# A decoder layer on one Trainium2 core: query norms by selector products, paired 64x64 products, and two sums moved off VectorE

## The chip, the core and the metric

The kernel runs on one core of one Trainium2 chip. The core has TensorE (PE in the profile, with its weight loads listed apart as PEld), VectorE (DVE), ScalarE (ACT), GpSimd (POOL) and a queue of DMA issues on SyncE (SP). The metric is the device time of one execution in microseconds; lower is better.

## The reference, cut to what matters

The layer takes x of 4 sequences with 512 tokens of width 512. It adds three parts to x, each after a layer norm: a gated delta-rule attention with 16 heads, a routed cross-attention over 64 context rows, and a feed-forward block with ternary weights. The change touches the first part alone:

```python
q = _causal_conv_silu(hidden_states @ Wq, conv_q).reshape(B, T, H, DK)   # DK = 96, 4 taps
k = _causal_conv_silu(hidden_states @ Wk, conv_k).reshape(B, T, H, DK)
v = _causal_conv_silu(hidden_states @ Wv, conv_v).reshape(B, T, H, DV)   # DV = 192
q = _l2norm(q) * DK ** (-0.5)                # divides by the root of the sum of squares
k = _l2norm(k)
...
def step(S, inp):                            # over 512 tokens, for every head
    q_t, k_t, v_t, g_t, b_t = inp
    S = S * jnp.exp(g_t)[..., None, None]
    kv = jnp.einsum('bhk,bhkv->bhv', k_t, S)
    delta = (v_t - kv) * b_t[..., None]
    S = S + jnp.einsum('bhk,bhv->bhkv', k_t, delta)
    o = jnp.einsum('bhk,bhkv->bhv', q_t, S)
    return (S, o)
...
o = o * jax.lax.rsqrt(var + EPS) * norm_weight * jax.nn.silu(gate)
return o.reshape(B, T, VAL_DIM) @ Wo         # and x = x + that
```

## The kernel before, in words

The attention is worked in 16 steps: 4 sequences, and for each of them 4 groups of 4 heads. The recurrence over tokens is done in 4 chunks of 128 tokens. Inside a chunk the delta rule is a triangular system, whose inverse is built once per step.

A step has these stages. `keys` projects the key channels of 4 heads in 3 tiles of 128 channels (96 of one head, and a third of the fourth head in the other 32), applies the four convolution taps and SiLU, transposes the keys to get their norms, and forms key-by-key products `lm`, masked by decays. `invert` inverts the triangular blocks: 32x32 blocks by substitution on VectorE (31 rounds of a product and a reduction), then the 32-wide and 64-wide off-diagonal blocks by small products on TensorE. `queries` projects the queries in the same way, takes their sums of squares (`ssq`) and forms key-by-query products. `pair` runs twice per step, each for two heads: `values` projects 3 value tiles, takes taps and SiLU, and turns them from channels to tokens by 32x32 transposes on VectorE, a store to DRAM and a load back; `gates` projects the gates; then the chunks follow in order, with the state in SBUF, and each chunk's output is normed, gated, turned through DRAM and multiplied by `Wo`, and the product is added to the residual tile `x`.

`project` is the helper of all convolved projections: four products of 128x512 in f32 accumulate in a PSUM bank, ScalarE writes the last tap's product to an `acc` tile, and VectorE adds the three other taps straight from PSUM.

Nothing is issued in the order of the source. Every operation is recorded by `Recorder.record` with an estimated cost and with its dependences, and `Recorder.order` plays the recorded operations through a list scheduler: for each engine it takes the ready operation that can start first, and among equals the one that is due first. Due times come from the step number (times `PERIOD`; keys and inversion of the next step count as `LEAD` steps later) and from a table `SHIFT` of offsets by stage and engine. Tiles live in numbered slots (6 for `acc`, 3 PSUM banks `mm`, 2 `tp`, 3 `ch`), and an operation that needs a slot waits in the plan till one is free. Operations in a `rec.group()` stay together. Then `emit` writes each engine's instructions in the planned order; on the chip each engine runs its own list strictly in that order. All these instructions carry line L558, where `emit` calls them, and so a line tells nothing here: groups are told apart by tile names and shapes.

`busywork` looks for gaps of TensorE in the plan that are longer than `IDLE` (0.8 us) and fills them with 128x128 products on a free PSUM bank, which nobody reads. They carry line L556.

```python
n = int((min(o.start - at, most) - IDLE) / each)
```

An f32 product shows as two PE instructions (two passes); a transpose as one.

Of the kernel before, what the change touches and what calls it, by code (L numbers as in the profile page):

```python
# [41 lines left out]
PERIOD = 133.9  # L42
LEAD = 6.21
PERIOD2 = 6.0
IDLE = 0.8
TERNARY = 7
# [3 lines left out]
    "ffn": -286.8,  # L50
    "ffn gpsimd": -630.6,
    "ffn scalar": 95.3,
    "ffn tensor": 9.6,
    "ffn vector": -751.6,
    "gate": -14.6,
    "gate scalar": 309.8,
    "gate tensor": 70.8,
    "head": -371.9,
    "head gpsimd": 602.6,
    "head scalar": 531.6,  # L60
    "head tensor": 307.0,
    "head vector": 293.4,
    "inv": 43.3,
    "inv gpsimd": -20.4,
    "inv scalar": -59.4,
    "inv tensor": -18.8,
    "inv vector": -64.7,
    "keys": 84.4,
    "keys gpsimd": 118.7,
    "keys scalar": 1126.6,  # L70
    "keys tensor": -205.3,
    "keys vector": -169.0,
    "out": 93.1,
    "out gpsimd": 163.4,
    "out scalar": 284.7,
    "out tensor": 136.0,
    "out vector": -605.5,
    "query": 22.7,
    "query gpsimd": -0.2,
    "query scalar": -194.1,  # L80
    "query tensor": -15.6,
    "query vector": -235.0,
    "rec": -229.1,
    "rec scalar": -429.1,
    "rec tensor": -1099.0,
    "rec vector": -319.3,
    "route": -26.3,
    "route gpsimd": 158.5,
    "route scalar": -304.1,
    "route tensor": -259.5,  # L90
    "route vector": 422.0,
    "tern": -187.4,
    "tern scalar": 56.9,
    "tern tensor": 115.4,
    "tern vector": 686.3,
    "value": -352.2,
    "value scalar": 287.9,
    "value tensor": -1023.7,
    "value vector": -417.0,
    "wo": 128.6,  # L100
    "wo scalar": -58.9,
# [200 lines left out]
class Op:  # L302
    __slots__ = ("engine", "calls", "cost", "tail", "deps", "nexts", "bufs", "due", "step", "table",
                 "waits", "start", "end", "index", "ready", "nbytes", "stage")


class Recorder:
# [18 lines left out]
    def group(self):  # L326
        return Group(self)

    def record(self, engine, method, args, kw):
        outs = [args[0]] + ([kw["accum_out"]] if "accum_out" in kw else [])  # L330
        ins = [x for x in list(args[1:]) + [v for k, v in kw.items() if k != "accum_out"]
               if isinstance(x, (View, bass.AP))]
        if self.grouped is not None and self.grouped.calls:
            op = self.grouped
            assert op.engine == engine
        else:
            op = self.grouped if self.grouped is not None else Op()
            op.engine, op.calls, op.cost, op.deps, op.nexts = engine, [], 0.0, set(), []
            op.bufs, op.step, op.table, op.index, op.nbytes = [], self.step, None, len(self.ops), 0
            op.stage = self.stage  # L340
            self.ops.append(op)
        op.calls.append((method, args, kw))
        op.cost += self.cost(op, engine, method, args, kw, outs, ins)
        for b in self.held:
            self.use(op, b)
        self.held = []
        ins += self.needed
        self.needed = []
        for x in ins:
            self.touch(op, x, False)  # L350
        for x in outs:

            self.touch(op, View(x.buf) if engine == "tensor" else x, True)
# [69 lines left out]
    def order(self, period, shift):  # L423
# [11 lines left out]
        for o in ops:  # L435
            o.due += shift.get(o.stage, 0.0) + shift.get(f"{o.stage} {o.engine}", 0.0)
# [87 lines left out]
    def busywork(self, banks, weights, moving, most=99.0):  # L524


        each = self.cost(None, "tensor", "matmul", (None, weights, moving), {}, [moving], [])
        use = {}
        for o in self.done:
            for b in o.bufs:  # L530
                if b.slots in banks:
                    t = use.setdefault((b.slots, b.slot), {}).setdefault(b, [o.start, o.end])
                    t[1] = max(t[1], o.end)
        fill, at = {}, 0.0
        for o in self.done:
            if o.engine != "tensor":
                continue
            n = int((min(o.start - at, most) - IDLE) / each)
            free = [k for k, u in use.items() if all(t[1] < at or o.start < t[0] for t in u.values())]
            if n > 0 and free:  # L540
                fill[o] = free[0][0].tiles[free[0][1]], n
            at = o.start + o.cost
        return fill
# [27 lines left out]
class Group:  # L571


    def __init__(self, rec):
        self.rec = rec
# [6 lines left out]
    def __exit__(self, *exc):  # L582
        self.rec.grouped = None
# [3 lines left out]
def decoder_layer(ctx: ExitStack, tc: tile.TileContext, a: dict, out: bass.AP):  # L587
# [7 lines left out]
    w.vs = dram.tile([NB, NHG, T, GV], F32, name="vs")  # L595
    w.os = dram.tile([NB, NHG, NC, GV, P], F32, name="os")
# [69 lines left out]
def attention(w, a):  # L666
# [38 lines left out]
    t_k = slots("k", 8, [DK, T])  # L705
    t_q = slots("q", 5, [DK, T])
# [13 lines left out]
    t_j = slots("j", 1, [P, NC * DK], ordered=False)  # L720
    t_oq = slots("oq", 1, [P, HG * DV])
# [99 lines left out]
    def project(wsrc, hT, taps):  # L821


        w = t_w(P, KC, P)
        sp.dma_start(w, wsrc)
        pp = p_mm(P, T)
        acc = t_acc(P, T)
        for kc in range(KC):
            rec.hold(acc)
            pe.matmul(pp, w[:, kc], hT[:, kc], start=kc == 0, stop=kc == KC - 1)  # L830
        act.activation(acc, pp, AF.Copy, scale=taps[:, 3:4])
        for j in range(1, 4):
            dve.scalar_tensor_tensor(
                acc[:, j:], pp[:, : T - j], taps[:, 3 - j : 4 - j], acc[:, j:], ALU.mult, ALU.add
            )
        return acc, w

    def project4(key, f, hT, taps, t_dst):


        dst = [t_dst(DK, T) for _ in range(4)]
        for i in range(3):
            rec.hold(*dst)
            acc, _ = project(a[key][f, i], hT, taps[:, i])
            act.activation(dst[i], acc[:DK], AF.Silu)
            act.activation(dst[3][32 * i : 32 * i + 32], acc[DK:P], AF.Silu)
        return dst

    def keys(s, f):
# [4 lines left out]
        k = project4("wk", f, s["hT"], cqk[:, 0, f], t_k)  # L854
# [3 lines left out]
        for j in range(4):  # L858
            pk = p_tp(P, NC, DK)
            rec.hold(kt[j])  # L860
            with rec.group():
                for c in range(NC):
                    pe.transpose(pk[:, c], k[j][:, c * P : (c + 1) * P], ident[:DK, :DK])
# [27 lines left out]
        for j in range(4):  # L891
            pa = p_tp(P, NC, P)
            rec.hold(lm)
            rec.need(dec[j])
            with rec.group():
                for c in range(NC):
                    cs = slice(c * P, (c + 1) * P)
                    pe.matmul(pa[:, c], k[j][:, cs], k[j][:, cs], start=True, stop=True)
            dve.tensor_tensor(lm[:, j], pa, dec[j], ALU.mult)
        return s  # L900

    def invert(s):
# [48 lines left out]
        for n0 in range(0, NPR, 8):  # L951
            p0 = p_tp(P, 8, 64)
            rec.hold(tb)
            with rec.group():
                for n in range(8):
                    pe.matmul(
                        p0[64:128, n], lm[0:64, n0 + n, 64:128], xa[:, n0 + n], start=True, stop=True
                    )
            act.copy(tb[64:128, n0 : n0 + 8], p0[64:128])
        for n0 in range(0, NPR, 8):  # L960
            p1 = p_tp(P, 8, 64)
            with rec.group():
                for n in range(8):
                    pe.matmul(
                        p1[0:64, n], tb[64:128, n0 + n], lm[64:128, n0 + n, 64:128], start=True, stop=True
                    )
            act.copy(lm[0:64, n0 : n0 + 8, 64:128], p1[0:64])

    def queries(s, f):

        rec.stage = "query"
        q = project4("wq", f, s["hT"], cqk[:, 1, f], t_q)
        s["q"] = q
        ssq = s["ssq"] = t_s(P, 4, NC)
        for j in range(4):
            pk = p_tp(P, NC, DK)
            with rec.group():
                for c in range(NC):
                    pe.transpose(pk[:, c], q[j][:, c * P : (c + 1) * P], ident[:DK, :DK])
# [4 lines left out]
        for j in range(4):  # L984
            pa = p_tp(P, NC, P)
            rec.need(s["lm"][:, j])
            with rec.group():
                for c in range(NC):
                    cs = slice(c * P, (c + 1) * P)
                    pe.matmul(pa[:, c], s["k"][j][:, cs], q[j][:, cs], start=True, stop=True)  # L990
            dve.tensor_tensor(s["dec"][j], pa, s["dec"][j], ALU.mult)

    def values(s, hg, jo):
# [3 lines left out]
        for vt in range(NVT):  # L997
            rec.hold(*vo)
            acc, w = project(a["wv"][hg, vt], s["hT"], cv[:, hg * NVT + vt])
# [29 lines left out]
    def pair(s, hg, jo, last):  # L1029
# [13 lines left out]
        for c in range(NC):  # L1043
# [3 lines left out]
            if c:  # L1047
                pr, rz = p_ch(P, HG, DV), t_rz(P, HG, DV)
                rec.hold(rz)
                for j in range(HG):  # L1050
                    pe.matmul(pr[:, j], k[jo + j][:, cs], st[:, j], start=True, stop=True)
# [25 lines left out]
            if c:  # L1077
                pq, oq = p_ch(P, HG, DV), t_oq(P, HG, DV)
                rec.hold(oq)
                for j in range(HG):  # L1080
                    pe.matmul(pq[:, j], q[jo + j][:, cs], st[:, j], start=True, stop=True)
# [39 lines left out]
            dve.tensor_add(x, x, py)  # L1121
# [326 lines left out]
def layouts(i):  # L1448
# [20 lines left out]
    def halves(wm):  # L1469
# [10 lines left out]
        "xid": substitution_start(),  # L1480
        "wv": by_tile(i[n + "Wv"], P).reshape(NHG, NVT, P, KC, P),
# [35 lines left out]
```

## Time and profile before

| what | value |
|---|---|
| median of 3 runs | 2442.74 us (2439.18 to 2442.87) |
| the profiled execution, its own time | 2443.09 us |
| its span, first to last instruction | 2441.3 us |
| mean granted TensorE clock | 0.988 |
| TensorE busy | 2354.8 us, 96% |
| VectorE busy | 1940.5 us, 79% |
| ScalarE busy | 1331.2 us, 55% |
| GpSimd busy | 856.3 us, 35% |
| filler products on L556 | 746 passes |

A group's line gives line, engine, operation, tiles out and in, shapes and count, then busy time and mean time of one, then the engine's idle time just before and what ended it. [...] The first 200 us are the start of the pipeline, the last 240 us are routing and feed-forward, and between them a step takes about 134 us.

### The profile page before, as it was taken

To read this page: it belongs to the slowest core of one execution; us is meant where nothing else is said; L and a number is where in the kernel's file an instruction comes from. 1 tells how busy PE (TensorE), PEld (TensorE's weight loads), DVE (VectorE), ACT (ScalarE), POOL (GpSimd) and SP (SyncE) were. 2 spreads that over 40 slices of the span, in tenths; PEclk is the share of its full clock that TensorE was granted. 3 is DMA by queue.
4 is the path that set the end of the run, shared out by engine and by line. 5 is a ranking of instruction groups with operands and counts; after the bars stand their busy time and mean duration, and the time that the engine had idled before them with its cause. 6 is when DMAs were issued, how large, how long until landed. Compare 5 with 4: busy or idle time off the path is not lost.

```text
span 2441.3 us, 38049 instructions
## 1 busy us (share of the span) xinstructions
PE 2354.8 (96%) x12976; PEld 1478.7 (61%) x12976; DVE 1940.5 (79%) x3594; ACT 1331.2 (55%) x2807; POOL 856.3 (35%) x1275
## 2 busy tenths in 40 slices
PE   8989999999999999999999999999999999999988
PEld 5576566666565756565664756665657575644455
DVE  4978797979696979788869889898979796587764
ACT  3746456555455575747553656455364554655553
POOL 2332333233333232314122333333223422376663
PEclk9989999999999999999999999999999999999999
DMA  5547343535353455556664545554544445431000
GB/s 167 148 117 192 84 114 74 129 82 159 90 156 90 129 145 149 146 154 163 163 171 104 142 111 137 152 146 127 153 125 118 112 110 157 115 81 60 22 18 18
DMA packets 579009, 294.76 MB, mean 121 GB/s; under 512 B 424000, under 2 KB 495936, under 8 KB 578560
## 3 DMA queue, kind: packets, MB, share of 16 engines
q1 hardware_dynamic: 578816, 292.34, 45.7%
q8 instruction: 103, 1.69, 0.3%
q14 instruction: 90, 0.74, 0.1%
HBM read 223.93 MB, written 68.29 MB: 120 GB/s over the span
## 4 chain that ended last, share of the span: by engine, by line
PE 72%; DVE 15%; ACT 6%; POOL 3%; issue 2%; DMA 1%; SPq 0%; POOLq 0%; DVEq 0%; ACTq 0%
PE mm L558 45%; PE ch L558 16%; DVE mem L558 15%; PE tp L558 10%; ACT mem L558 5%; POOL mem L558 3%; ACT L558 1%; PE tp L556 1%; DMA vs<-mem 0%; PE ch L556 0%; DMA mem<-vs 0%; SPq L558 0%; DMA mem<-in_wg 0%; DMA mem<-in_cst 0%; PE mm L556 0%
## 5 line engine op out<-in xcount | busy, mean ns | idle before, releaser
L558 PE MATMUL mm<-mem 128*128 128x512 f32 (+4 forms) x3760 | 1527.1, 543 | 20.1 <-issue 6.7
L558 PEld LDWEIGHTS mm<-mem 128*128 128x128 f32 (+1 forms) x3504 | 627.2, 190 | 536.5 <-issue 399.0
L558 POOL TENSOR_TENSOR mem<-mem 128x2 f32<-128x2 f32 (+5 forms) x864 | 714.3, 839 | 671.5 <-ACT mem L558 464.5
L558 ACT ACTIVATE mem<-mem 128x192 f32<-128x192 f32 (+6 forms) x1361 | 674.4, 524 | 454.9 <-DVE mem L558 307.0
L558 DVE SCALAR_TENSOR_TENSOR mem<-mm,mem 128x511 f32<-128x511 f32 (+4 forms) x656 | 463.5, 728 | 168.2 <-ACT mem L558 144.3
L558 PE MATMUL ch<-mem 128*128 128x192 f32 (+3 forms) x2688 | 547.9, 342 | 30.8 <-DVE mem L558 18.9
L558 PEld LDWEIGHTS ch<-mem 128*128 128x128 f32 (+2 forms) x2176 | 367.1, 188 | 151.0 <-issue 44.2
L558 PEld LDWEIGHTS tp<-mem 32*32 32x32 f32 (+3 forms) x5462 | 322.3, 137 | 137.4 <-issue 61.2
L558 PE MATMUL tp<-mem 32*32 32x32 f32 (+7 forms) x5782 | 371.5, 225 | 23.9 <-ACT mem L558 15.0
L558 DVE TENSOR_REDUCE mem<-mem 128x4 f32<-128x384 f32 (+32 forms) x660 | 332.7, 506 | 64.2 <-POOL mem L558 33.5
L558 POOL TENSOR_SCALAR mem<-mem 128x1 f32<-128x1 f32 (+3 forms) x352 | 121.3, 345 | 576.3 <-ACT mem L558 378.5
L558 DVE STREAM_TRANSPOSE mem<-mem 128x384 f32<-128x384 f32 (+3 forms) x368 | 279.8, 763 | 50.9 <-ACT mem L558 24.0
L558 DVE TENSOR_TENSOR mem<-mem 128x64 f32<-128x64 f32 (+31 forms) x553 | 250.2, 454 | 16.5 <-POOL mem L558 1.9
L558 ACT ACTIVATE mem<-mm,mem 128x512 f32<-128x512 f32 x192 | 130.1, 682 | 189.0 <-PE mm L558 188.0
L558 ACT COPY mem<-tp 32x512 f32<-32x512 f32 (+6 forms) x292 | 172.3, 603 | 83.7 <-PE tp L558 80.8
L558 DVE SCALAR_TENSOR_TENSOR mem<-ch,mem 128x192 f32<-128x192 f32 (+1 forms) x272 | 128.4, 508 | 49.9 <-PE ch L558 44.9
L558 PEld LDWEIGHTS <-mem 128*128 128x128 bf16 x1088 | 92.1, 98 | 119.9 <-ACT mem L558 16.7
L558 ACT ACT_TABLE_LOAD x114 | 146.3, 1283 | 30.1 <-DVE mem L558 27.6
L558 DVE TENSOR_TENSOR mem<-mem,mm 128x512 f32<-128x512 f32 x144 | 97.0, 678 | 46.5 <-PE mm L558 44.7
L558 DVE TENSOR_TENSOR mem<-tp,mem 128x512 f32<-128x512 f32 (+1 forms) x132 | 87.0, 666 | 44.0 <-PE tp L558 26.6
L558 ACT COPY mem<-ch 128x384 f32<-128x384 f32 x128 | 60.8, 475 | 92.6 <-PE ch L558 91.9
L558 ACT ACTIVATE mem<-mm 128x384 f32<-128x384 f32 x128 | 61.9, 488 | 84.2 <-PE mm L558 83.5
(33 smaller groups left out, 772.6 us busy)
## 6 DMA issues: line engine op xcount, KB each, us to landing
mem<-in_wg SPq DMA_DIRECT2D x32, 768.0 KB, 4.6
mem<-in_wv SPq DMA_DIRECT2D x96, 256.0 KB, 3.0
mem<-wos SPq DMA_DIRECT2D x96, 256.0 KB, 3.2
vs<-mem SPq DMA_DIRECT2D x384, 64.0 KB, 2.7
mem<-vs SPq DMA_DIRECT2D x128, 192.0 KB, 3.5
os<-mem SPq DMA_DIRECT2D x512, 48.0 KB, 2.6
mem<-os SPq DMA_DIRECT2D x128, 192.0 KB, 2.9
mem<-gs SPq DMA_DIRECT2D x64, 256.0 KB, 4.7
```

The source lines that it names most:

```text
L556: engine.matmul(bank[:, : m.shape[1]], w, m, start=True, stop=True)
L558: getattr(engine, method)(*[real(x) for x in args], **{k: real(v) for k, v in kw.items()})
```

## The change

Four edits to the computation's placement, and a new plan.

1. Query norms: the query tiles are no longer transposed for their sums of squares. ScalarE squares the three projected tiles in place, three products with a 128x32 selector `sel` (ones in column 0 for the first 96 rows, in column 1 for the last 32) sum over channels on TensorE, each into its own 32 rows of one PSUM bank, and the sums go to DRAM and come back with tokens on partitions.
2. The four groups of eight 64x64 products in `invert` become three: the middle one interleaves the second product of the first half with the first product of the second half.
3. In the value projections (`F = 1`) the tap of offset 3 is multiplied by ScalarE out of PSUM into the weight tile and added by GpSimd, in place of VectorE's third tap.
4. The product with `Wo` is copied out of PSUM by ScalarE and added to `x` by GpSimd (`HP = 1`).

A group may now state its cost for the planner; `SHIFT` has entries by stage, engine and output tile; `PERIOD`, `LEAD` and all offsets are other numbers; and no filler is put ahead of TensorE's first operation. The SiLU of the first three key and query tiles now covers all 128 rows.

```diff
-PERIOD = 133.9
-LEAD = 6.21
+PERIOD = 137.5
+LEAD = 10.97
+QN = 1
+F = 1
+HP = 1
 ...
-            n = int((min(o.start - at, most) - IDLE) / each)
+            n = int((min(o.start - at, most) - IDLE) / each) if at else 0
 ...
     def __exit__(self, *exc):
+        if self.cost is not None:
+            self.rec.grouped.cost = self.cost
 ...
-    def project(wsrc, hT, taps):
+    def project(wsrc, hT, taps, split=False):
 ...
         act.activation(acc, pp, AF.Copy, scale=taps[:, 3:4])
-        for j in range(1, 4):
+        if split:
+            last = w.rearrange("p k c -> p (k c)")
+            act.activation(last[:, 3:], pp[:, : T - 3], AF.Copy, scale=taps[:, 0:1])
+        for j in range(1, 3 if split else 4):
             dve.scalar_tensor_tensor(
                 acc[:, j:], pp[:, : T - j], taps[:, 3 - j : 4 - j], acc[:, j:], ALU.mult, ALU.add
             )
+        if split:
+            pool.tensor_add(acc[:, 3:], acc[:, 3:], last[:, 3:])
 ...
-            acc, _ = project(a[key][f, i], hT, taps[:, i])
-            act.activation(dst[i], acc[:DK], AF.Silu)
+            acc, _ = project(a[key][f, i], hT, taps[:, i], F > 1 and key == "wq" or F > 2)
+            act.activation(dst[i], acc, AF.Silu)
 ...
-        for n0 in range(0, NPR, 8):
-            p0 = p_tp(P, 8, 64)
-            with rec.group():
-                for n in range(8):
-                    pe.matmul(
-                        p0[64:128, n], lm[0:64, n0 + n, 64:128], xa[:, n0 + n], start=True, stop=True
-                    )
-            act.copy(tb[64:128, n0 : n0 + 8], p0[64:128])
-        for n0 in range(0, NPR, 8):
-            p1 = p_tp(P, 8, 64)
-            with rec.group():
-                for n in range(8):
-                    pe.matmul(
-                        p1[0:64, n], tb[64:128, n0 + n], lm[64:128, n0 + n, 64:128], start=True, stop=True
-                    )
-            act.copy(lm[0:64, n0 : n0 + 8, 64:128], p1[0:64])
+        for n0 in (0, 8, 16):
+            pi = p_tp(P, 8, 64)
+            with rec.group(0.94):
+                for n in range(8):
+                    if n0 < NPR:
+                        m = n0 + n
+                        pe.matmul(pi[64:128, n], lm[0:64, m, 64:128], xa[:, m], start=True, stop=True)
+                    if n0:
+                        m = n0 - 8 + n
+                        pe.matmul(
+                            pi[0:64, n], tb[64:128, m], lm[64:128, m, 64:128], start=True, stop=True
+                        )
+            if n0 < NPR:
+                act.copy(tb[64:128, n0 : n0 + 8], pi[64:128])
+            if n0:
+                act.copy(lm[0:64, n0 - 8 : n0, 64:128], pi[0:64])
 ...
+        if QN:
+            pq = p_tp(P, T)
+            for i in range(3):
+                act.activation(accs[i], q[i], AF.Square)
+            with rec.group(0.9):
+                for i in range(3):
+                    pe.matmul(pq[32 * i : 32 * i + 32], sel, accs[i], start=True, stop=True)
+            act.copy(accs[0][:DK], pq[:DK])
+            there = w.qs[s["b"], f]
+            for i in range(3):
+                sp.dma_start(there[2 * i : 2 * i + 2], accs[0][32 * i : 32 * i + 2])
+            sums = t_sums(P, 3, 2, NC)
+            for i in range(3):
+                sp.dma_start(sums[:, i], there[2 * i : 2 * i + 2].rearrange("h (c p) -> p h c", p=P))
+            dve.tensor_copy(ssq[:, 0:3], sums[:, :, 0])
+            dve.tensor_reduce(ssq[:, 3], sums[:, :, 1].rearrange("p i c -> p c i"), AX.X, ALU.add)
-        for j in range(4):
+        for j in range(0 if QN else 4):
 ...
-            acc, w = project(a["wv"][hg, vt], s["hT"], cv[:, hg * NVT + vt])
+            acc, w = project(a["wv"][hg, vt], s["hT"], cv[:, hg * NVT + vt], F > 0)
 ...
-            dve.tensor_add(x, x, py)
+            if HP:
+                y = t_acc(P, D)
+                act.copy(y, py)
+                pool.tensor_add(x, x, y)
+            else:
+                dve.tensor_add(x, x, py)
```

## The prediction, made before the changed kernel ran

> **What bounds the kernel now.** I read the page's busy times and slices first, then the answer by stretches, the groups with shapes kept apart, the waits of TensorE (PE), and last the timeline of single groups.
>
> ```profile
> span 2441.3 us, 38049 instructions
> PE 2354.8 (96%) x12976; PEld 1478.7 (61%) x12976; DVE 1940.5 (79%) x3594; ACT 1331.2 (55%) x2807; POOL 856.3 (35%) x1275
> PE 72%; DVE 15%; ACT 6%; POOL 3%; issue 2%; DMA 1%; SPq 0%; POOLq 0%; DVEq 0%; ACTq 0%
> ```
>
> PE is busy for 96% of the span and holds 72% of the chain that ended last; VectorE (DVE) comes second, ScalarE (ACT) and GpSimd (POOL) have room. The stretches (length, then busy us of PE, weight load, DVE, ACT, POOL; clock) show the shape:
>
> ```profile
> 60.00:194.00 134.00, 122.05 (x820) 92.28 (x819) 118.55 (x212) 84.67 (x160) 51.15 (x59) 0.94 0.48 137
> 596.00:730.00 134.00, 132.69 (x716) 80.86 (x717) 104.38 (x192) 69.45 (x153) 42.63 (x64) 1.00 0.46 117
> 1266.00:1400.00 134.00, 123.68 (x682) 79.85 (x682) 115.61 (x217) 68.89 (x152) 41.46 (x55) 0.96 0.46 118
> ```
>
> A step in the middle is PE alone: 1.3 us of 134 are idle. The first step and a dip at 1266 lose 10 to 12 us each. Part of "busy" is filler (L556: products nobody reads, put where the planner sees a gap). The filler alone, by start, middle, end:
>
> ```profile
> 0.00:200.00 200.00, 34.70 (x266) 33.72 (x266) 0.94 0.49 146
> 200.00:2200.00 2000.00, 28.78 (x210) 27.15 (x210) 0.99 0.50 129
> 2200.00:2442.00 242.00, 32.69 (x270) 31.72 (x270) 1.00 0.09 30
> ```
>
> 746 filler passes, 96 us. All of DVE's 1940 us can therefore shrink without moving the end by more than what PE waits for DVE:
>
> ```profile
> PE ch L558 <- DVE mem L558: 18.9, 20, 4.6
> PE tp L558 <- ACT mem L558: 15.0, 28, 1.9
> PE ch L558 <- ACT mem L558: 10.8, 18, 1.3
> PE tp L558 <- DVE mem L558: 7.8, 11, 1.2
> ```
>
> With two smaller lines (mm after ACT 6.6, after DVE 4.8) that is 31.5 us behind DVE and 32.4 us behind ACT, of 2441.
>
> **PE's own work.** The pace comes from timeline rows, since listed durations overlap (start, length, count):
>
> ```profile
> 41.75 0.50 PE L558 MATMUL tp<-mem 96*128 96x96 f32 x4
> 1109.28 1.20 PE L558 MATMUL tp<-mem 32*32 32x32 f32 x64
> 1110.41 7.13 PE L558 MATMUL mm<-mem 128*128 128x512 f32 x16
> 1120.63 1.11 PE L558 MATMUL tp<-mem 64*64 64x64 f32 x16 [0.67 <-ACT mem L558]
> 1342.99 2.17 PE L556 MATMUL tp<-mem 128*128 128x128 f32 x18
> ```
>
> Take one listed duration off the length and divide by the steps. A 512-wide pass: (7.13-0.60)/15 = 0.435 us; an f32 product is two passes. A 96-row transpose (one pass): (0.50-0.25)/3 = 0.083. A 64x64 pass: (1.11-0.22)/15 = 0.059, so a group of 8 products 0.94. A filler pass: (2.17-0.27)/17 = 0.112. A 32x32 pass, with products on two different corners of the array taking turns: (1.20-0.19)/63 = 0.016; single starts there come in couples 7 ns apart, 24 ns between couples. The second pass of one product thus runs beside the first pass of the next, and starts stay in order.
>
> 1. Query norms. 16 transposes a step go: 256 x 0.083 = -21.2 us. Added: three products 32 columns wide, 512 long, on three column groups, x16. No row shows this form. Fully side by side they take 2 x 0.435 = 0.87 us, one after another 2.61. By the corner rows (a pass of one beside a pass of the next, in order) it is 4 passes, 1.74 us. I take 1.74: +27.8 us (ends 13.9 and 41.8). [...] Entering and leaving the narrow form: the product after the 64x64 group starts 0.09 us late, x32 = +2.9 (ends 0 and 6).
> 2. Pairing. Four groups of 8 become 8, 16 interleaved, 8 on opposite corners. By the corner rows the interleaved 16 take about as long as 8 alone: -0.94 x 16 = -15.0 us (ends -16 and 0). The price: the second half's first product now waits in one group with the first half's second; its cover is the next step's projections, as now.
> 3. Filler. In the emitted order of the changed program I count 900 passes against 746: start 164 (266), middle 516 (210), end 220 (270). Difference +154 x 0.112 = +17.2 us. The 82 at the very start go; cold, they took 10.98 us, not 9.2: -1.6. The cold clock then falls on real work instead: +2. In the middle alone it is +34 us, with two runs of 55 and 80 products ahead of a pair's output products and recurrence. There the planner gave PE nothing else; the step's chain (taps, sum, SiLU, turn, store, load, scale) has to be waited out.
> 4. DVE's work, cost by the groups (count | busy, mean ns of one):
>
> ```profile
> L558 DVE SCALAR_TENSOR_TENSOR mem<-mm,mem 128x509 f32<-128x509 f32 x192 | 139.0, 741 | 3.9
> L558 DVE TENSOR_TENSOR mem<-mem,mm 128x512 f32<-128x512 f32 x144 | 97.0, 678 | 46.5 <-PE mm L558 44.7
> L558 POOL TENSOR_TENSOR mem<-mem 128x512 f32<-128x512 f32 x208 | 247.1, 1218 | 75.2 <-DVE mem L558 73.3 <-ACT mem L558 1.4
> L558 ACT ACTIVATE mem<-mm,mem 128x512 f32<-128x512 f32 x192 | 130.1, 682 | 189.0 <-PE mm L558 188.0
> ```
>
> DVE loses 96 taps x 0.741 = 71, 128 residual sums x 0.678 = 87, 64 query reductions x 0.547 = 35; 32 small ones come (0.2 each): -187 us, to 72%. ACT gains 96 x 0.682 = 65, 128 copies x 0.581 = 74, 16 copies = 9; its squares change from 64 x 0.488 to 48 x 0.649 (even); 19 table loads fewer x 1.283 = -24: +124, to 60%. POOL gains 224 x 1.218 = +273, to 46%. All this is hidden by PE, except in PE's waits. DVE's wait of 31.5 us falls with its load; between the first step (DVE 88%, PE idle 12) and a middle step (78%, idle 1.3) it falls faster than the load, so I take a quarter: -8. ACT's 32.4 grows by its 9%: +3. Bounds: -31 and +30.
>
> [...]
>
> ```profile
> L558 DVE TENSOR_TENSOR mem<-mem 128x480 f32<-128x480 f32 x16 | 12.1, 753 | 0.5
> ```
>
> This takes 753 ns where the 512-wide one with a PSUM input takes 678, about 108 over its size, with POOL's wide sums on 20% of the span; the change makes that 32%. [...]
>
> 5. Queues. SP issues 97 more DMAs at 0.43 us: 42 us of a queue that waits most of the time. The three loads of norms carry 1024 four-byte pieces each; four-byte packets take 9 ns here, so 192 per engine are 1.7 us a step, ahead of value loads. Behind SP's wait for the norms' copy stand value stores. POOL's new sum waits for both ACT and DVE, and behind it stand the gates and norms of the output stage; DVE's turn waits for it through SiLU. On a value tile's chain that is one ACT pass off DVE's 0.74 and 1.2 more on POOL, +0.5 us a tile, hidden behind two or three tiles in flight.
> 6. A lower row count for slots (accumulators kept for squares and residual copies, 6 in all) shows in the emitted order as the filler of point 3; not counted twice.
>
> Sum: -21.2 + 27.8 + 2.9 - 15.0 + 17.2 - 1.6 + 2 - 8 + 3 = +7.1. Span 2441.3 + 7.1 = 2448.4; the profiled execution took 2443.09, 1.8 more than its span (the median shown is 2442.74, 0.35 less than it): 2450.2, I say 2450. PE's net saving is 5 us where the planner's costs (0.168 a transpose, 0.9 for the three narrow products) promise far more, and the middle's filler eats it.
>
> **Rivals.**
> A. DVE's waits go. Place: recurrence products behind DVE (18.9 us) and the first step, where 81 fillers and then 2 us of waiting stand ahead of the inversion. If three quarters of 31.5 us vanish (-24 in place of -8) and the first step sheds another 12 us of idle PE to look like a middle step, it is 2450 - 16 - 12 = 2422. For it: DVE is 88% busy where PE idles most, and the start has 102 filler passes fewer. Against: in the middle PE has only 45 us idle in 2000, and 306 filler passes (34 us) are added there. It decides from 12 us of relief on beyond my 5, where the result passes 2438.
> B. The value chain becomes the bound: POOL's sum stands behind gate and norm work in a strict order, and each of 32 pairs enters its recurrence 1.2 us later with nothing for PE to do: +38, 2488. For it: those two long filler runs say PE already runs out of work there. Against: POOL at 46%.
> C. The narrow products overlap fully: -14, 2436; or not at all: +14, 2464. Small either way, and inside the forecast's range.
> That the change doesn't do what it says: the emitted order shows all four parts, 256 transposes fewer and 48 narrow products.
>
> **Numbers.** Runs differ by 0.15%, so 0.2% (4.9 us: 2437.9 to 2447.6) is what a measurement can tell. Forecast with C around it: 0.54, own range 2436 to 2466, of which slower 0.41, same 0.10, faster 0.03. A: 0.34, faster 0.31, same 0.03. B: 0.12, slower. Together: faster 0.34, same 0.13, slower 0.53. Both signs weigh, so the range runs from A's far side, 2412, to B's near side, 2484.
>
> **What would show it.** Right: PE still at 96%; 16 groups of six narrow passes of about 1.7 us; interleaved 64x64 passes near 0.03 us apart; filler 900 passes and near 110 us, more in the middle; DVE near 1750, ACT near 1455, POOL near 1130. A is right if PE's waits behind DVE fall under 10 us and a stretch from 60 to 194 has PE over 128. B is right if PE waits behind ACT or DMA for over 60 us ahead of recurrence products. Wrong as a whole: middle steps of 130 us or less, or narrow groups over 2.6 us.

## The result, and the profile after

The changed kernel takes 2498.86 us (median; 2494.19 to 2500.04) against 2442.8 for the kernel before: ratio 1.0229, 95% interval 1.0211 to 1.0247. The forecast had the sign and not the size: 2450, with a range to 2484. The page of the changed kernel (its real instructions carry line L675, the filler L673):

```profile
span 2492.4 us, 38312 instructions
...
PE 2368.0 (95%) x12970; PEld 1467.0 (59%) x12970; DVE 1809.1 (73%) x3338; ACT 1432.0 (57%) x3012; POOL 1153.5 (46%) x1499
...
PE 39%; DVE 15%; ACT 5%; POOL 3%; issue 2%; DMA 1%; SPq 0%; POOLq 0%; DVEq 0%; ACTq 0%
```

ACT and POOL are near the forecast (1455 and 1130). DVE is 59 us above it (1750): it was relieved of 131 us, not 187. The shares of the chain add up to 65% only, so it was followed through a part of the span and is not read further. Here are the same three stretches as before (length, then busy us of PE, weight load, DVE, ACT, POOL; clock, DMA share, GB/s):

```profile
60.00:194.00 134.00, 121.47 (x793) 87.85 (x792) 117.29 (x230) 88.59 (x182) 55.15 (x66) 0.97 0.54 146
596.00:730.00 134.00, 130.03 (x716) 81.56 (x716) 92.55 (x170) 75.48 (x166) 56.01 (x68) 0.99 0.48 121
1266.00:1400.00 134.00, 124.04 (x692) 78.96 (x692) 115.70 (x209) 76.03 (x167) 58.89 (x69) 0.97 0.54 134
```

PE's idle time in the middle step rises from 1.3 to 4.0 us while DVE's work there falls by 12. PE idles more behind an engine that has less to do. The waits of PE say behind which engine (total us, times, longest; `ch`, `tp` and `mm` are the PSUM banks that PE writes):

```profile
PE ch L675 <- DVE mem L675: 44.7, 34, 5.3
PE tp L675 <- DVE mem L675: 17.7, 14, 7.6
PE ch L675 <- ACT mem L675: 13.7, 26, 0.7
...
PE mm L675 <- DVE mem L675: 9.9, 13, 2.0
```

Behind DVE it is 72.3 us instead of 31.5; behind ACT (with 10.6 for tp and 8.0 for mm) 32.3 instead of 32.4. The filler alone, as before in start, middle and end, has the 900 passes that were counted:

```profile
0.00:200.00 200.00, 20.16 (x164) 19.27 (x164) 0.98 0.56 163
200.00:2200.00 2000.00, 60.41 (x506) 59.67 (x506) 0.98 0.50 126
2200.00:2494.00 294.00, 27.89 (x230) 27.13 (x230) 1.00 0.12 39
```

PE's own edited work, from the timeline (start, length; x6 means that six passes are merged in one row):

```profile
98.00 1.06 PE L675 MATMUL tp<-mem 128*32 128x512 f32 x6
98.99 0.91 PE L675 MATMUL mm<-mem 128*128 128x384 f32 x2
```

and the 64x64 products among the groups with shapes apart:

```profile
L675 PE MATMUL tp<-mem 64*64 64x64 f32 x1024 | 55.2, 221 | 0.8 <-ACT mem L675 0.8
```

Six narrow passes are through after 0.99 us: the three first passes start within 14 ns, the three second ones 0.45 us later. Start to start, the 48 narrow products take 16.4 us in all, 1.03 a step (0.99 in 15 steps, 1.60 in the last).

**Where a state copy waits.** Timeline of the changed kernel, where PE's longest wait behind a recurrence sum lies:

```profile
1066.16 3.22 POOL L675 TENSOR_TENSOR mem<-mem 128x512 f32<-128x512 f32 x2 [14.69 <-ACT mem L675]
...
1067.32 0.94 DVE L675 TENSOR_TENSOR mem<-mem 128x432 f32<-128x432 f32 x1
...
1068.93 0.94 DVE L675 TENSOR_TENSOR mem<-mem 128x448 f32<-128x448 f32 x1
...
1070.56 0.64 DVE L675 TENSOR_TENSOR mem<-mem 128x464 f32<-128x464 f32 x1
...
1074.70 0.69 DVE L675 TENSOR_TENSOR mem<-mem 128x512 f32<-128x512 f32 x1
1075.31 1.01 DVE L675 COPY mem<-ch 96x384 f32<-96x384 f32 x2
...
1075.92 1.33 PE L675 MATMUL ch<-mem 96*128 96x192 f32 x3 [5.29 <-DVE mem L675]
```

Two things are to be seen. PE has waited 5.29 us for the copy of the state, which stands in DVE's strict order behind rounds of the next step's substitution. And under GpSimd's two sums (1066.16 to 1069.38) a round's product takes 0.94 us; after them a larger one takes 0.64. The stretch makes only some 0.6 us of this wait of 5.29, an estimate from these rows. I paired all SBUF products of DVE with what GpSimd did beside them. Against the fast fifth (20th percentile) of their own shapes they are 407 ns longer where a 128x512 GpSimd sum covers most of them (51 products), 420 under a 128x384 one (26), and 0 with GpSimd idle (311). Sums out of PSUM, reductions and transposes hardly move (5, 2 and 20 ns under the 128x512 sums; 4, 4 and 20 with GpSimd idle). Summed over all of DVE's instructions, the time above that floor is 70 us before and 98 after; that is the excess in what follows.

**Planned and late.** The kernel's own planner gives each operation a start. I paired DVE's instructions in order with the profile. "Plan" is the planner's last end in us, "late" the median of profile start less planned start over the last 60 instructions. The kernel before: plan 2397, late 44. The changed one: plan 2403, late 90. The lateness grows by 5 to 19 us per 200 us of plan, up to 1600. So the loss is 6 us of plan and 46 us of running late against it. The experiments are to say why.

### The profile page after: what moved, and what is told of

Read it like the earlier page. It is cut to its first block, busy times and chain, and to the rows that moved or that the text cites. A ratio compares the mean times of both kernels' runs of the same rounds, so it can differ in the third digit from the quotient of the medians.

```text
span 2492.4 us, 38312 instructions
## 1 busy us (share of the span) xinstructions
PE 2368.0 (95%) x12970; PEld 1467.0 (59%) x12970; DVE 1809.1 (73%) x3338; ACT 1432.0 (57%) x3012; POOL 1153.5 (46%) x1499
## 4 chain that ended last, share of the span: by engine, by line
PE 39%; DVE 15%; ACT 5%; POOL 3%; issue 2%; DMA 1%; SPq 0%; POOLq 0%; DVEq 0%; ACTq 0%
PE mm L675 24%; DVE mem L675 15%; PE ch L675 10%; PE tp L675 5%; ACT mem L675 4%; POOL mem L675 3%; SPq L675 0%; ACT L675 0%; DMA mem<-qs 0%; PE tp L673 0%; DMA mem<-vs 0%; DMA mem<-gs 0%; DMA mem<-wos 0%; DMA mem<-os 0%; DMA vs<-mem 0%
## 5 line engine op out<-in xcount | busy, mean ns | idle before, releaser
L675 PE MATMUL mm<-mem 128*128 128x512 f32 (+5 forms) x3760 | 1522.6, 544 | 32.0 <-DVE mem L675 9.9
L675 POOL TENSOR_TENSOR mem<-mem 128x512 f32<-128x512 f32 (+4 forms) x1088 | 1010.2, 943 | 838.2 <-ACT mem L675 541.9
L675 PEld LDWEIGHTS mm<-mem 128*128 128x128 f32 (+2 forms) x3504 | 631.9, 191 | 576.1 <-issue 429.1
L675 ACT ACTIVATE mem<-mem 128x192 f32<-128x192 f32 (+4 forms) x1409 | 702.8, 527 | 461.2 <-POOL mem L675 211.6
L675 PE MATMUL ch<-mem 128*128 128x192 f32 (+3 forms) x2688 | 554.6, 347 | 58.9 <-DVE mem L675 44.7
L675 DVE SCALAR_TENSOR_TENSOR mem<-mm,mem 128x511 f32<-128x511 f32 (+4 forms) x560 | 396.7, 728 | 270.5 <-ACT mem L675 251.3
L675 PEld LDWEIGHTS ch<-mem 128*128 128x128 f32 (+2 forms) x2176 | 372.4, 191 | 174.4 <-DVE mem L675 72.2
L675 PE MATMUL tp<-mem 32*32 32x32 f32 (+7 forms) x5622 | 345.2, 230 | 29.6 <-DVE mem L675 17.7
L675 PEld LDWEIGHTS tp<-mem 32*32 32x32 f32 (+4 forms) x5302 | 284.1, 136 | 143.0 <-issue 61.1
L675 DVE STREAM_TRANSPOSE mem<-mem 128x384 f32<-128x384 f32 (+3 forms) x368 | 280.7, 764 | 90.5 <-POOL mem L675 53.0
L675 DVE TENSOR_REDUCE mem<-mem 128x4 f32<-128x384 f32 (+25 forms) x612 | 301.7, 494 | 35.5 <-POOL mem L675 17.1
L675 POOL TENSOR_SCALAR mem<-mem 128x1 f32<-128x1 f32 (+3 forms) x352 | 123.3, 351 | 359.4 <-ACT mem L675 281.6
L675 ACT ACTIVATE mem<-mm,mem 128x512 f32<-128x512 f32 (+1 forms) x288 | 187.1, 682 | 168.2 <-PE mm L675 162.6
L675 DVE TENSOR_TENSOR mem<-mem 128x64 f32<-128x64 f32 (+31 forms) x553 | 268.9, 487 | 17.2 <-POOL mem L675 1.9
L675 ACT COPY mem<-tp 32x512 f32<-32x512 f32 (+7 forms) x308 | 181.1, 603 | 91.7 <-PE tp L675 88.4
L675 DVE SCALAR_TENSOR_TENSOR mem<-ch,mem 128x192 f32<-128x192 f32 (+1 forms) x272 | 128.0, 507 | 75.6 <-PE ch L675 66.3
L675 PEld LDWEIGHTS <-mem 128*128 128x128 bf16 x1088 | 92.2, 98 | 119.6 <-issue 19.5
L675 ACT COPY mem<-mm 128x512 f32<-128x512 f32 (+1 forms) x144 | 77.9, 545 | 86.2 <-PE mm L675 85.3
L675 ACT COPY mem<-ch 128x384 f32<-128x384 f32 x128 | 61.0, 476 | 103.0 <-PE ch L675 102.1
L675 DVE TENSOR_TENSOR mem<-tp,mem 128x512 f32<-128x512 f32 (+1 forms) x132 | 86.0, 665 | 33.7 <-PE tp L675 32.9
L675 DVE TENSOR_SCALAR mem<-mem 128x512 bf16<-128x512 f32 (+3 forms) x178 | 75.9, 436 | 42.0 <-POOL mem L675 16.8
```

The lines of the kernel that those rows point to most:

```text
L675: getattr(engine, method)(*[real(x) for x in args], **{k: real(v) for k, v in kw.items()})
```

## Experiments

Every ratio is to runs of the kernel before on the same chip. "Planned anew" means that the list was ordered again for the variant; "fixed order" that the order of the kernel named is kept and only the instructions of the edit differ. The kernel before took 2439.2 to 2442.8 us on these chips, so a difference between two variants is known to some 4 us; it is given by the times, with the one by the ratios where that differs.

**1. Which part loses, planned anew.** Eight variants of the changed kernel:

```diff
 e1_old_plan:         PERIOD, LEAD, SHIFT of the kernel before, all edits kept
 e2_plan_only:        QN = F = HP = 0 under the new numbers (pairing kept)
 e3_filler_cap:       -most=99.0  +most=3.0   in busywork
 e4_old_ternary:      the "tern" entries of SHIFT from the kernel before
 e5_no_residual:      -HP = 1  +HP = 0
 e6_no_value_split:   -F = 1   +F = 0
 e7_no_selector:      -QN = 1  +QN = 0
 e8_pairing_only:     numbers of the kernel before, QN = F = HP = 0, pairing kept
```

> All four edits, but PERIOD, LEAD and SHIFT of the kernel before. Theory P (the plan's new numbers put too much of other work ahead of two recurrences, and the edits themselves gain PE 23 us): 2420 to 2455. Theory E (the edits themselves, ScalarE and above all GpSimd on the value and residual paths, cost the time): 2480 or more.

> The new plan numbers and the pairing, but query norms, value taps and residual sums done as before. Theory P: 2480 or more, with long filler again between 1000 and 1250 us. Theory E: 2440 or less.

> The changed kernel with each run of filler cut to 10 products or fewer (a gap counts for at most 3 us); the order of all other work is the same. If the filler itself is the loss (its data there before it ends): 35 to 45 us less, about 2460. If it only stands in real waits, as theories P and E have it: 0 to 12 us less, or more if the clock falls, about 2490 to 2502; the run of 80 ended 5 us after the value load that it waited for.

> The changed kernel with the kernel before's SHIFT entries for the ternary weights alone. In the changed kernel these stores run from 965 to 1554 us, before from 1000 to 1806. If their crowding is the loss of steps 7 and 8 (theory P in its narrow form): 2450 to 2465, and the step from the fourteenth to the seventeenth state copy gets 40 us shorter. If not: within 12 us of 2499.

> The changed kernel with the residual's sum again on VectorE out of PSUM (HP = 0); planned anew with the same numbers. So far: the edits cost 22 us under the new numbers (2499 against 2477) and TensorE's waits of recurrence products behind VectorE are 45 us with them, 19 without. Theory G (GpSimd's wide sums put VectorE late: by the residual above all, 128 of 224): 2475 to 2485, those waits under 30 us. If the value taps are the cause: 2495 or more, waits still over 40.

> The changed kernel with all three value taps on VectorE (F = 0). Theory V (GpSimd's sum lengthens the value chain and VectorE's turn waits for it, in strict order ahead of recurrence work): 2475 to 2485, waits of recurrence products behind VectorE under 30 us. If the residual is the cause: 2495 or more.

> The changed kernel with query norms by transposes as before (QN = 0). TensorE's own work rises by 12 us (24.6 us of transposes for 16.4 us of narrow products and their switches). If the norms are harmless: 2500 to 2515. If their slots and loads are what hurts the plan: 2485 or less.

> The kernel before with its own plan numbers, and of the change the paired 64x64 products and the missing first filler alone. TensorE's own work falls by 11 us and the first transposes start 10 us earlier. If the plan's numbers survive such an edit: 2420 to 2436. If any edit upsets numbers that were fitted to another program, as the 53 us of the ternary entries suggest: 2450 or more.

| kernel | residual sum on | us | ratio, 95% interval | plan | late |
|---|---|---|---|---|---|
| before | DVE | 2442.8 | 1 | 2397 | 44 |
| after | GpSimd | 2498.9 | 1.0229 (1.0211 to 1.0247) | 2403 | 90 |
| e1_old_plan | GpSimd | 2604.3 | 1.0671 (1.0653 to 1.0688) | 2501 | 100 |
| e2_plan_only | DVE | 2477.2 | 1.0145 (1.0128 to 1.0162) | 2454 | 21 |
| e3_filler_cap | GpSimd | 2505.1 | 1.0264 (1.0247 to 1.0281) | 2403 | 96 |
| e4_old_ternary | GpSimd | 2552.3 | 1.0449 (1.0431 to 1.0466) | 2450 | 102 |
| e5_no_residual | DVE | 2515.4 | 1.0299 (1.0273 to 1.0326) | 2479 | 37 |
| e6_no_value_split | GpSimd | 2567.3 | 1.0511 (1.0490 to 1.0531) | 2476 | 94 |
| e7_no_selector | GpSimd | 2550.0 | 1.0447 (1.0429 to 1.0465) | 2468 | 79 |
| e8_pairing_only | DVE | 2470.2 | 1.0118 (1.0101 to 1.0135) | 2430 | 35 |

Read by time alone the table says nothing: whatever is taken out, and whatever numbers are put in, every variant is slower than the kernel before, and the theory that the numbers lose and the edits gain falls as well as its opposite. e2, e3 (by 3 us), e4 and e7 lie in neither of the bands expected, and e5 (2515) is far above what its theory asked. Read by columns, the table says two things. The plan ends 33 to 104 us later than that of the kernel before, except in the changed kernel and with the cap (6 us), as it would with offsets that were fitted to one program. And the lateness falls into two groups: 79 to 102 us with the residual sum on GpSimd, 21 to 44 without. DVE's excess falls into the same two, 87 to 99 us and 62 to 70. Only e5 differs from the changed kernel by the sum alone, and it was planned anew, so this shows where to look and not yet a cause. The filler is innocent: capped, its time comes back as waits (PE's ch products behind DVE 58.4 instead of 44.7), and the mean granted clock falls from 0.985 to 0.971. With the ternary loads where they were (e4) the time is longer.

**2. Is a new plan alone worth so much?** The kernel before with one offset nudged:

```diff
-    "query": 22.7,
+    "query": 23.7,
```

> The kernel before with one number changed, the offset of the query stage from 22.7 to 23.7 us; every instruction is the same, the list is planned anew. Its planner's own end moves from 2397 to 2433 us (for the changed kernel eight such nudges leave it at 2403). If a new plan alone moves the time as the plan says: 2433 plus the 44 us of lateness of the kernel before, 2465 to 2490; then differences of this size between variants planned anew tell nothing of an edit. If the planned end means nothing: 2435 to 2450.

Measured 2481.46 us, ratio 1.0163 (1.0143 to 1.0183). The page:

```profile
span 2479.3 us, 38353 instructions
...
PE 2380.0 (96%) x13136; PEld 1499.4 (60%) x13136; DVE 1940.1 (78%) x3594; ACT 1324.7 (53%) x2802; POOL 854.7 (34%) x1275
```

The work of DVE, ACT and POOL is that of the kernel before (within 7 us), and 160 more filler passes stand on PE. The plan foretold it: 2433, with 46 us of lateness. So 42 us can come of the order alone, and from here on the order is kept.

**3. Each moved sum undone at the changed kernel's own order.** In `emit`, ScalarE's and GpSimd's instructions of the edit are not issued, and VectorE's old one is put back:

```diff
 f1_residual_fixed
-                act.copy(y, py)
-                pool.tensor_add(x, x, y)
+                dve.tensor_add(x, x, py)            # where the copy stood
 f2_value_tap_fixed
-            act.activation(last[:, 3:], pp[:, : T - 3], AF.Copy, scale=taps[:, 0:1])
-            pool.tensor_add(acc[:, 3:], acc[:, 3:], last[:, 3:])
+            dve.scalar_tensor_tensor(acc[:, 3:], pp[:, : T - 3], taps[:, 0:1], acc[:, 3:], ...)
```

> The changed kernel with its planned order kept instruction for instruction, except that the residual's sum is one VectorE add out of PSUM again, put where ScalarE's copy stood in the order; ScalarE's copy and GpSimd's add are not issued. Nothing else moves, so no re-planning hides in the number. For each kernel the times at which its list planner thought each VectorE instruction would start were set against the profile: the kernel before ends 44 us later than planned, the changed one 90, the two variants with the old residual sum under the new offsets 21 and 37, those with the new sum 79 to 102. Theory L (the residual's way over ScalarE and GpSimd makes the run late against its plan): lateness falls by 30 to 50 us although VectorE works 128 x 0.68 = 87 us more, time 2440 to 2470. Theory E (the instructions of the edits gain at a given order, and only the planned order costs): VectorE's 87 us in its strict order makes PE wait more for the recurrence's sums, 2510 to 2550, the waits of the 96x192 products behind VectorE 60 us or more.

> The changed kernel with its order kept, except that the last tap of the value convolutions is the third VectorE sum again, directly behind the second; ScalarE's product and GpSimd's sum of it are not issued (96 of each). Theory E: VectorE works 96 x 0.75 = 72 us more in a strict order that has no room for it, 2505 to 2540. Theory L (lateness comes of the residual alone): within 10 us of the changed kernel, 2490 to 2510. If the value chain over GpSimd was what costs (the second rival of the forecast), 2450 to 2475.

f1: 2512.26 us, 1.0292 (1.0275 to 1.0310). f2: 2508.81 us, 1.0281 (1.0262 to 1.0300). At the given order each edit therefore gains, 13 and 10 us (15 and 13 by the ratios), for 87 and 72 us of DVE's work. That is far below what each takes off DVE. The theory that the residual on GpSimd only loses falls in this form, and so does the lateness as a mark of it: f1 runs 114 us late with the sum on DVE, in an order that has no place for it. DVE's excess is 73 us in f1 and 91 in f2, against 98: the residual sums make 25 of it, the value taps' 96 sums 7. What the residual sum costs at this order is still open.

**4. The recurrence first.** Rounds of the substitution planned within 4 us ahead of a recurrence sum are emitted just behind it:

```diff
+        self.defer(4)     # new: DVE's [rounds..., recurrence sum] is emitted as [recurrence sum, rounds...]
```

> The changed kernel with one thing moved in VectorE's order: rounds of the substitution that the plan put within 4 us ahead of a recurrence sum (the state's copy and sums, and the corrected values) are emitted just behind it; no instruction is added or taken away, nothing is planned anew. Theory R (the loss is PE's products waiting for recurrence sums that stand behind substitution rounds): the waits of the 96x192 products behind VectorE go from 45 to 10 to 20 us, time 2445 to 2475. Rival: VectorE then waits idle for PE's products in its strict order, and the substitution comes late instead (GpSimd and ScalarE behind VectorE rise), 2490 to 2530.

> The same move on the kernel before (rounds within 4 us ahead of a recurrence sum go behind it), nothing else changed. Its 96x192 products wait 19 us behind VectorE. Theory R: 2425 to 2440, a little faster than the kernel before. Rival (the substitution's delay costs as much): 2440 to 2475.

f3 on the changed kernel: 2539.68 us, 1.0404 (1.0387 to 1.0422). f4 on the kernel before: 2532.81 us, 1.0381 (1.0364 to 1.0398). PE's waits in f3:

```profile
PE ch L697 <- DVE mem L697: 51.7, 59, 2.7
PE ch L697 <- ACT mem L697: 24.2, 36, 2.0
```

Both runs are slower than either of their bands. The longest wait halves (5.3 to 2.7 us), but there are 59 instead of 34, and DVE's own waits for PE's ch products rise from 132.5 to 195.4 us: it now stands idle where it did rounds before. So an earlier place of the copy is no cure for the wait in the timeline above.

**5. The residual sum's own price.** GpSimd's 128 sums are left out (g1), or replaced by two writes of zeros that keep GpSimd busy and waiting in the same place (g2):

```diff
 g1_no_residual_sum:   -pool.tensor_add(x, x, y)
 g2_residual_memset:   -pool.tensor_add(x, x, y)   +pool.memset(y, 0.0)   +pool.memset(y, 0.0)
```

> The changed kernel in its own order, with GpSimd's 128 residual sums left out (part of the computation: the products of wo are copied out of PSUM and added to nothing). GpSimd works 128 x 1.27 = 163 us less; nothing else is changed. In the trace of the changed kernel a VectorE product of two SBUF operands takes 838 ns where a 128x512 GpSimd sum covers it and 401 where GpSimd is idle, sums out of PSUM do not change. Theory G (the residual sums on GpSimd are what makes the run late, through the stretched VectorE products or through waits for GpSimd): 2440 to 2465. Rival (they are hidden, the lateness is the order's own): 2485 to 2500.

> As the run before, but in the place of each residual sum GpSimd writes zeros twice into the copied tile (about 2 x 0.5 us): GpSimd stays busy and waits for ScalarE's copy as before, but reads no two SBUF operands. The residual's sum is left out. If the stretching of VectorE's products is what costs, as fast as the run without the sums; if GpSimd's time and waits are what costs, 2485 to 2500 as the changed kernel; if the run without the sums is not faster, neither.

g1: 2472.42 us, 1.0133 (1.0114 to 1.0151). g2: 2469.05 us, 1.0122 (1.0105 to 1.0139). g2's page, then its group of writes (shapes apart), then PE's waits (L676 is the changed kernel's L675):

```profile
PE 2353.1 (96%) x12970; PEld 1459.5 (59%) x12970; DVE 1782.3 (72%) x3338; ACT 1432.3 (58%) x3012; POOL 1115.4 (45%) x1627
```

```profile
L676 POOL MEMSET mem<- 128x512 f32 x256 | 133.8, 527 | 180.3 <-ACT mem L676 172.8
```

```profile
PE ch L676 <- DVE mem L676: 30.7, 27, 3.6
```

g1 lies between its two bands; g2 is as fast as g1. GpSimd is nearly as full in g2 as in the changed kernel (1115 us against 1154), and yet 30 us go (26 in g1; by the ratios 26 and 23). Under these writes DVE's products are 8 ns longer (47 of them), not 407. DVE is busy 27 us less with the same 3338 instructions, its excess falls from 98 to 73, PE's ch waits fall by 14, the lateness from 90 to 60. So it is not GpSimd's time or its place in the chain: 23 to 30 us of the loss come of the sums as sums, and the stretch of DVE's products is what goes with them.

One rival is left by the edit: in g1 and g2 the 16 stores of `x` don't wait for GpSimd either. The waits of the DMA queue on SP behind GpSimd do fall, from 34.6 to 8.2 us. But it hardly reaches the engines: PE (with its weight loads), DVE, ACT and POOL together wait for DMAs 90 us in the changed kernel and 89 in g2. g1 also gives the price of the sum at this order: on GpSimd it costs 26 us, on VectorE (f1, without ScalarE's copies) 40, so the edit gains although it stretches.

**6. Is any DVE time worth that much?** The last three of 31 rounds are left out:

```diff
-        for t in range(1, BS):      # product and reduction
+        for t in range(1, 29):      # in the emitted order; planned as before
```

> The changed kernel in its own order, without the last three of the substitution's 31 rounds (part of the computation left out): 4.2 us less of VectorE in each of 16 steps, 67 us in all. Theory S (the substitution's chain on VectorE is what the plan's critical line runs through, since rounds moved back by up to 4 us cost 41 us on this kernel and 90 on the one before, while 87 us of VectorE's residual sums in the same order cost 13): 40 us or more faster, below 2460. Rival (any VectorE work is worth the same at this order, 0.15 us per us): 2485 to 2495.

g3: 2483.22 us, 1.0173 (1.0156 to 1.0190): 16 us (14 by the ratios) for 67 us of DVE's instructions, about a quarter; the profile has DVE busy 56 us less. The theory that the substitution's chain sets the pace (40 us or more) falls. Time taken from this place is largely absorbed; 27 us of stretching cost about their whole length. Why the stretching weighs more was not tried.

**7. The value tap at the order before.** ScalarE's and GpSimd's halves, and ScalarE's alone:

```diff
 g4_value_tap_before   (the kernel before, fixed order)
+            act.activation(last[:, 3:], pp[:, : T - 3], AF.Copy, scale=taps[:, 0:1])
-            dve.scalar_tensor_tensor(acc[:, 3:], ...)     # third tap
+            pool.tensor_add(acc[:, 3:], acc[:, 3:], last[:, 3:])
 h2_only_scalar_product: the first of these lines alone
```

> The kernel before in its own order, with the last tap of the value convolutions by ScalarE and GpSimd (ScalarE's product directly behind its first one, GpSimd's sum where the third VectorE sum stood, 96 of each). Nothing planned anew. Theory E (the edits gain at a given order: 10 us for this one in the changed kernel's): 2428 to 2440. Rival (the order before was made for VectorE's sum and GpSimd stands in other waits): 2445 to 2475.

> The kernel before in its own order with only ScalarE's half of the value tap: 96 ScalarE products of 0.68 us directly behind the first one, written where nobody reads them, VectorE keeps its third sum and GpSimd gets none. With GpSimd's half as well the run was 57 us slower than the kernel before. If ScalarE's place in its strict order is what costs there (PE's waits behind ScalarE rose from 32 to 52 us): 2480 to 2510, VectorE's 72 us more included. If the way over GpSimd costs: 2440 to 2460.

g4: 2496.62 us, 1.0226 (1.0207 to 1.0244). h2: 2462.67 us, 1.0098 (1.0074 to 1.0123). The waits of PE, ACT and DVE in g4:

```profile
PE tp L559 <- ACT mem L559: 28.2, 34, 3.2
PE tp L559 <- DVE mem L559: 19.6, 23, 2.1
PE ch L559 <- DVE mem L559: 18.9, 19, 4.6
...
ACT mem L559 <- POOL mem L559: 255.9, 154, 12.2
...
DVE mem L559 <- ACT mem L559: 321.0, 198, 15.5
```

The edit that gains 10 us in the order made for it costs 57 in the other: 23 by ScalarE's products in its strict order, where nothing was relieved, and 34 more by the way over GpSimd, although DVE then has 72 us less. My expectation of a gain was wrong, g4 is slower than its rival's band too, and h2 missed both of its bands. The stretch doesn't explain the 34: DVE's excess is 77 us in g4 and 66 in h2. The chain does more: ACT's waits for GpSimd rise from 93.0 us in h2 to 255.9, DVE's for ACT from 232.7 to 321.0, and PE's tp waits behind DVE from 9.4 to 19.6. That is the way of the second rival of the forecast (sum, SiLU, turn), in an order that was made without it; how much of the 34 us it makes was not tried. None of the kernels tried is faster than the kernel before.

## Why the prediction was wrong, step by step

- Steps 1 and 2, mis-sized. The narrow products take 1.03 us a step, not 1.74. In turn they would be 2.61, worked out from six passes of 0.435, so they run 2.5 times faster. The corner rows, of products that differ in rows and columns alike, were the wrong nearest row. Start to start and without PE's waits, the transposes fell by 24.2 us (forecast 21.2) and the 64x64 groups by 14.3 (forecast 15.0). PE's own work fell by 22 us, not by 5.5: -16.6 against the sum.
- Step 3 held: 900 passes, 17 us by their usual distance. TensorE's slow start is in both traces: before, filler passes start 213 ns apart up to 9.9 us of the span and 112 from 10.1 on; in the changed kernel real 128x512 passes start 0.85 us apart up to 16.1 us of the span and 0.43 from 16.8 on.
- Step 4 failed, in the term "so I take a quarter: -8". PE's waits behind DVE rose by 41. The term behind ACT (+3) was 0. The premise was that a wait falls with the load of the engine waited for. DVE's load fell and PE's wait behind it rose; what rose with the wait is the lateness against the plan. One sign stood in the rows of before: the substitution's 128x480 product took 753 ns, an estimated 108 over its size, with POOL's wide sums on 20% of the span; the sum has no term for it. DVE's excess grew by 28 us, g2 puts its busy time 27 us lower, and PE's work doesn't cover it: g1 and g2 show 23 to 30 us of the time.
- Step 5 held for the norms' queue: DVE waits 6.5 us in all for those loads. The +0.5 us a value tile stayed hidden here (f2, without the split, is slower), though g4 points to it in another order.
- The clock was left out beyond the start: 0.985 against 0.988 of the span is 36 us short of full speed against 29, +7. This is an estimate and an upper one: by the same reckoning e3 would lose 37 us more than the changed kernel, and its span is 11 longer.

The forecast's +7.1, corrected by -16.6, +49 and -3 for the waits and up to +7 for the clock, gives at most +43.5 of the +51.1 us of span measured; 7.6 or more stay unplaced. Of the 41 us of new waits, g2 takes off 14, nearly all in the ch products; its clock of 0.991 is worth up to 14 more by the reckoning above, of 29.5 us of span. The other 27 us of new waits, and g2's 16 us of lateness above the kernel before, are open. The value taps' sums are of the same kind, but the 7 us of excess that goes with them in f2 is too little.

The sign was luck. With the narrow products at their measured size and the waits as forecast, the sum is -9.5 us, a faster kernel.

Rival A (waits go) had the direction of DVE's load right and the waits wrong. Rival B gave nearly the measured time (2488) for a reason that this order doesn't show: PE's waits behind ACT and DMA are 37 us, not over 60. Rival C's overlap is nearly what happened, worth 11 of its 14 us, and was outweighed.

## What to carry to other kernels

Where an order is fixed beforehand, time is the plan's end plus the lateness against it: split a result into the two before blaming an edit, and undo an edit at a fixed order, since one re-planned offset moved this kernel by 42 us. But an order made for an edit also favours it: the value tap gained 10 us in its own order and cost 57 in the other. Work moved off VectorE to GpSimd was not all off VectorE here: under a GpSimd sum of two SBUF operands a VectorE product of two SBUF operands took 407 ns longer (51 products), under GpSimd's writes of zeros 8 ns (47). Don't price the stretch at nothing because some other engine's work seems to cover it; here, with 27 us of DVE's busy time, it cost about its full length (23 to 30 us in g1 and g2). And when a busy engine gets less to do and the engine behind it waits more, look also for what makes single instructions longer, not for load alone.

## What the runs showed of the hardware that was not expected

- Three f32 products of 32 columns and length 512 on three column groups start 6 to 7 ns apart and take 1.03 us together, against 2.61 in turn (six passes of 0.435, worked out).
- A GpSimd sum of two SBUF operands lengthened a VectorE product of two SBUF operands that it covered by about 0.4 us (407 ns on 51 products), here about doubling it; GpSimd's writes of zeros lengthened it by 8 ns, and its short operations on 128x2 not at all (53 products under them).
- With less filler the granted clock was lower: with each run of filler cut to what fits 3 us (e3), its mean was 0.971 instead of 0.985, and the time rose by 6 us only.
